# Two attention layers on one core: in the first image's first layer, the residual goes through TensorE and ScalarE, and the last merge of the exponential sums into the column sums

## The chip, the cores and the metric

The kernel runs on one core of a Trainium2 chip. The metric is device time in microseconds (us) for one launch. TensorE is called PE here, its weight loads PEld, VectorE DVE, ScalarE ACT, GpSimd POOL and the DMA queue's engine SP, as in the profile.

## The reference

The input x is four images of 128 channels and 4096 positions, in float32. Two attention layers follow one another; cut to what matters:

```python
# layer 0 (IC = 64), n positions, b images
g = g_w @ x + g_b;  theta = theta_w @ x + theta_b;  phi = phi_w @ x + phi_b
f = softmax(theta^T phi)                # over the keys, 4096 x 4096 per image
x = W_w @ (f @ g) + W_b + x             # residual
# layer 1 (C = 128)
q, k, v = Wq @ x + bq, Wk @ x + bk, Wv @ x + bv
x = x + softmax(q^T k / sqrt(C)) @ v    # residual
```

## The kernel before

Everything stays in float32. The queries of a layer and image are cut into 8 chunks of 512 positions, so there are 64 chunks in all. Their order is the list `chunks`: first the 8 chunks of layer 0 of image 0 (chunks 0 to 7), then chunks of layer 0 of the next image and of layer 1 of the present one by turns. Only the first 8 run with nothing but layer 0 around them.

A chunk takes the 4096 keys in 16 pairs of 128-key tiles. One pair of one chunk is a *slot* t of a software pipeline written out by hand (`slot(t)` under a manual schedule): each engine runs its instructions in the order in which the program issues them. A *turn* is 16 slots. In slot t the program issues, in this order:

- the scores of pair t (PE, L246 for layer 0, into one of two PSUM buffers `ps` of two banks), their copy to an SBUF tile `s` (ACT, L253), the exponential of pair t - 19 in place (ACT, L294), the running sum of that pair's exponentials into `sum` (POOL, L306 for the first addition, L308 for the others), the subtraction of the row maxima from pair t - 18 (DVE, L290), and the running maximum of pair t (DVE, L262, L260 for the first);
- in the odd slots, the value products of two pairs, 20 and 21 slots back (PE, L343 for layer 0);
- the work that comes once per chunk: in slot 0 of the next turn the merge of the maxima (DVE, L265), in slot 1 their transposition, column maximum and spreading (PE L270, DVE L275, PE L282). Chunk g's tail is in turn g + 2: the accumulated values leave PSUM in slot 4 (ACT, L360); `sum_columns` multiplies the exponential sums by a column of ones in slot 7 (PE, `pc`) and `invert` takes the reciprocal (DVE, L373); `sum_spread` and `normalize` are in slot 9 (PE `o_rc`, DVE L381), `project_out` and `residual` in slot 11 (PE `po`, DVE L393). The query projection of a coming chunk is in slot 13 (PE `pq`, ACT L233). `pc`, `o_rc`, `po` and `pq` share one PSUM bank, tag "m".

In the last slots of chunk 7 and after it, the keys and values of the next image (`pk`, `pv`) and of layer 1 come in between.

The exponential sums of a chunk are kept for the two key tiles of a pair side by side, a tile of 128 x 2 x 512. After the last pair, POOL adds the two halves (L311), and `sum_columns` reads only the first half.

`cut` (L187) issues a product as two halves of 64 output columns each when the mode of the slot is "col". While layer 0 is in PE's array the mode is "col", so all of the first eight chunks' `pc` and `po` products are issued in halves. PE's records of a float32 product are two for each half: one `po` is 4 records, one chunk's `pc` (4 blocks of 128 queries) 16.

Scores of layer 0 multiply on 64 rows for each tile of the pair, two products side by side in the array.

Of the kernel before, what the change touches and what calls it, by code (L numbers as in the profile page):

```python
# [11 lines left out]
AF = mybir.ActivationFunctionType  # L12
ALU = mybir.AluOpType
# [4 lines left out]
def kernel(  # L18
# [39 lines left out]
    nc = tc.nc  # L58
    B, C, N = x.shape
    IC = thT.shape[1]  # L60
    P = 128
    NB = 512
    NCH = N // NB
    KT = NB // P
    NPR = N // (2 * P)
# [17 lines left out]
    def const(name, shape):  # L83
        return cp.tile(shape, F32, tag=name, name=name)

    X = {}

    def load(b, j):
        t = xp.tile([C, NB], F32, tag="x", name=f"x_{b}_{j}")
        nc.sync.dma_start(out=t, in_=x[b, :, ts(j, NB)])  # L90
        X[b, j] = t

    ones = const("ones", [P, P])
    nc.gpsimd.memset(ones, 1.0)
    ident = const("ident", [P, P])
# [3 lines left out]
    wq0, wo0 = const("wq0", [P, P]), const("wo0", [P, P])  # L99
    wk0, wv0 = const("wk0", [P, IC]), const("wv0", [P, IC])  # L100
    bq0, bk0 = const("bq0", [P, 1]), const("bk0", [P, 1])
    g0, bo0, wb0 = const("g0", [IC, 1]), const("bo0", [P, 1]), const("wb0", [P, 1])
# [57 lines left out]
    chunks = [(0, 0, c) for c in range(NCH)]  # L160
# [5 lines left out]
    NG = len(chunks)  # L166
# [16 lines left out]
    def cut(out, lhsT, rhs, start=True, stop=True):  # L183

        cols = [slice(0, IC), slice(IC, P)] if now[0] == "col" else [slice(0, P)]
        for c in cols:
            nc.tensor.matmul(out[c], lhsT=lhsT[:, c], rhs=rhs, start=start, stop=stop)  # L187
# [7 lines left out]
    ACC = {}  # L195
    SUM = {}
# [99 lines left out]
    def own(g, p):  # L296

        return g == NG - 1 and p > 0 and p % 3 == 0
# [3 lines left out]
    def sums(g, p):  # L302
        s = S[g, p]
        if p == 1:
            SUM[g] = w2.tile([P, 2, NB], F32, tag="sum", name=f"sum_{g}")
            nc.gpsimd.tensor_tensor(SUM[g], S[g, 0], s, ALU.add)  # L306
        elif p > 1 and not own(g, p):
            nc.gpsimd.tensor_tensor(SUM[g], SUM[g], s, ALU.add)  # L308
        if p == NPR - 1 and g < NG - 1:
            t = SUM[g]  # L310
            nc.gpsimd.tensor_tensor(t[:, 0, :], t[:, 0, :], t[:, 1, :], ALU.add)  # L311

# [17 lines left out]
    def values(g, p):  # L330
# [8 lines left out]
        for h in range(2):  # L339
# [15 lines left out]
            else:  # L355
                nc.tensor.matmul(ACC[g], lhsT=v, rhs=s[:, h, :], start=first, stop=last)  # L356

    def leave(g):
        y = w2.tile([P, NB], F32, tag="y", name=f"y_{g}")
        nc.scalar.copy(y, ACC.pop(g))  # L360
        if g in HI:
            nc.vector.tensor_tensor(y, HI.pop(g)[0], y, ALU.add)
        ACC[g] = y

    def sum_columns(g):
        pc = ps_m.tile([P, KT], F32, tag="m", name=f"pc_{g}")
        for i in range(KT):
            cut(pc[:, i : i + 1], SUM[g][:, 0, ts(i, P)], ones[:, 0:1])
        SUM[g] = pc

    def invert(g):
# [11 lines left out]
    def project_out(g):  # L383
        if chunks[g][0] == 0:
            po = ps_m.tile([P, NB], F32, tag="m", name=f"po_{g}")
            cut(po, wo0, ACC[g])
            ACC[g] = po

    def residual(g):
        layer, b, c = chunks[g]  # L390
        if layer == 0:
            t = X[b, c]
            nc.vector.scalar_tensor_tensor(t, ACC.pop(g), bo0, t, ALU.add, ALU.add)  # L393
        else:
            t = X.pop((b, c))
            nc.vector.scalar_tensor_tensor(t, ACC.pop(g), bv1, t, ALU.add, ALU.add)
            nc.sync.dma_start(out=out[b, :, ts(c, NB)], in_=t)
            if loads:
                load(*loads.pop(0))
# [49 lines left out]
    def slot(t):  # L449
# [6 lines left out]
        if p == 4 and f is not None:  # L456
            leave(f)
        run(scores, of(t, 0))
        run(copy, of(t, 0))
        run(exps, of(t, EL))  # L460
        run(sums, of(t, EL))
        run(subtract, of(t, SL))
        if p == 1 and m is not None:
# [5 lines left out]
        def finish():  # L469
            if t in cols:  # L470
                sum_columns(cols[t])
                invert(cols[t])
            if t in spreads:
                sum_spread(spreads[t])
                normalize(spreads[t])
            if t in outs:
                project_out(outs[t])
                residual(outs[t])
            if t in queries:
                proj_q(queries[t])  # L480
# [56 lines left out]
```

## Time and profile before

| | |
|---|---|
| median of 3 runs | 3079.7 us (3072.96 to 3080.42) |
| profiled execution, its own time | 3076.04 us |
| its span, first to last instruction | 3074.3 us, granted TensorE clock 0.998 |
| PE busy | 3019.3 us, 98% of the span |
| DVE busy | 2532.6 us, 82% |
| ACT busy | 2096.9 us, 68% |
| POOL busy | 2383.8 us, 78% |
| residual of layer 0 (L393) on DVE | 32 in all, 742 ns each (median); those of chunks 0 to 7 start at 109.9 us and later |
| merge of the two halves of the sums (L311) on POOL | 63 in all, 1275 ns each (mean) |

Durations are from one profiled execution. A record's duration includes what overlaps with the next instruction of its engine, so the pitch from start to start is the time that it takes in a row of work. A window query gives the busy time of each engine in a stretch of the span; a wait is listed by who waited for whom, with the total, the number of times and the longest; a line of the timeline has start, duration, engine, source line, operation, output and inputs with shapes, count, and in brackets the idle time before it with its releaser.

### The profile page before, as it was taken

The page shows a single profiled execution, that of the slowest core. Times are in us where ns is not written, and L with a number is a line of the kernel's source. Part 1 is how long each engine was busy: PE and PEld are TensorE (multiplying, and loading weights), DVE is VectorE, ACT ScalarE, POOL GpSimd, SP SyncE. Part 2 cuts the span into 40 slices and gives each one's busy share as a digit, 9 for nine tenths or more (in the row PEclk, how much of TensorE's full clock was granted, in tenths as well). Part 3 has the DMA queues.
Part 4 walks back from the last instruction along what each step waited for, and adds up shares of the span by engine and source line. Part 5 has one row for each costly group of instructions (what it writes and reads, how often), then busy time and mean ns, then how long its engine had stood idle before and what let it go on. Part 6 is the DMA issues. An engine that isn't in the chain of part 4 may idle for free.

```text
span 3074.3 us, 35878 instructions
## 1 busy us (share of the span) xinstructions
PE 3019.3 (98%) x13484; PEld 1243.5 (40%) x13484; DVE 2532.6 (82%) x2337; ACT 2096.9 (68%) x2306; POOL 2383.8 (78%) x1025
## 2 busy tenths in 40 slices
PE   8999999999999999999999999999999999999998
PEld 3222343344443444433344444444333444444444
DVE  6999878888888788888888877888888886766677
ACT  6888867666667676776666776667766676555554
POOL 3999878777888677887878877788878776666667
PEclk9999999999999999999999999999999999999999
DMA  2000000000000000000000000000000000000000
GB/s 67 1 1 1 1 1 8 8 8 4 4 8 8 8 8 1 8 8 8 7 6 2 8 4 4 4 1 4 4 4 4 4 0 4 4 4 7 4 4 11
DMA packets 11534, 19.47 MB, mean 6 GB/s; under 512 B 2656, under 2 KB 3168, under 8 KB 11360
## 3 DMA queue, kind: packets, MB, share of 16 engines
q1 hardware_dynamic: 10896, 17.14, 1.7%
q8 instruction: 106, 1.74, 0.2%
q14 instruction: 68, 0.56, 0.1%
q10 hardware_dynamic: 464, 0.03, 0.0%
HBM read 8.79 MB, written 8.39 MB: 6 GB/s over the span
## 4 chain that ended last, share of the span: by engine, by line
PE 88%; DVE 6%; issue 3%; ACT 3%; POOL 1%; ACTq 0%; DVEq 0%; POOLq 0%
PE ps L187 29%; PE acc L351 15%; PE acc L356 12%; PE ps L246 11%; PE acc L343 11%; DVE mx L262 5%; PE pq L187 2%; ACT s L253 2%; PE pv L187 1%; PE pc L187 1%; PE pt L270 1%; PE o_mx L282 1%; DVE s L290 1%; PE o_rc L282 1%; PE po L187 1%
## 5 line engine op out<-in xcount | busy, mean ns | idle before, releaser
L308 POOL TENSOR_TENSOR sum<-sum,s 128x1024 f32<-128x1024 f32 x891 | 2150.6, 2414 | 494.5 <-ACT s L294 450.9
L253 ACT COPY s<-ps 128x1024 f32<-128x1024 f32 x1024 | 1032.2, 1008 | 853.7 <-PE ps L187 560.4
L262 DVE TENSOR_TENSOR mx<-ps,mx 128x1024 f32<-128x1024 f32 x896 | 1093.9, 1221 | 417.6 <-ACT s L253 417.0
L290 DVE TENSOR_TENSOR s<-s,o_mx 128x1024 f32<-128x1024 f32 x1024 | 1233.2, 1210 | 15.1 <-PE o_mx L282 13.3
L294 ACT ACTIVATE s<-s 128x1024 f32<-128x1024 f32 x1024 | 1090.0, 1065 | 16.5 <-DVE s L290 16.1
L187 PE MATMUL ps<-q,k 128*64 128x512 f32 (+1 forms) x3232 | 929.5, 594 | 2.8 <-ACT k L217 2.8
L246 PE MATMUL ps<-q,k 64*128 64x512 f32 x2048 | 519.3, 613 | 25.4 <-DVE mx L262 24.1
L187 PEld LDWEIGHTS ps<-q,k 128*64 128x64 f32 (+1 forms) x3232 | 325.5, 151 | 506.3 <-issue 445.0
L343 PE MATMUL acc<-s,v 128*64 128x512 f32 x2048 | 497.8, 601 | 8.7 <-ACT s L294 8.7
L352 PE MATMUL hi<-s,v 64*128 64x512 f32 x1104 | 496.0, 589 | 0.0
L351 PE MATMUL acc<-s,v 64*128 64x512 f32 x1104 | 496.0, 589 | 0.0
L356 PE MATMUL acc<-s,v 128*128 128x512 f32 x944 | 424.8, 593 | 0.8 <-ACT y L360 0.7
L351 PEld LDWEIGHTS acc<-s,v 64*128 64x128 f32 x1104 | 205.9, 187 | 260.7 <-issue 202.7
L246 PEld LDWEIGHTS ps<-q,k 64*128 64x128 f32 x2048 | 179.6, 186 | 299.9 <-DVE mx L262 149.1
L306 POOL TENSOR_TENSOR sum<-s,s 128x1024 f32<-128x1024 f32 x64 | 152.1, 2376 | 180.8 <-ACT s L294 180.5
L356 PEld LDWEIGHTS acc<-s,v 128*128 128x128 f32 x944 | 175.3, 190 | 203.3 <-issue 187.4
L343 PEld LDWEIGHTS acc<-s,v 128*64 128x64 f32 x2048 | 131.0, 136 | 279.7 <-issue 157.0
L352 PEld LDWEIGHTS hi<-s,v 64*128 64x128 f32 x1104 | 205.9, 187 | 0.0
L260 DVE TENSOR_TENSOR mx<-ps,s 128x1024 f32<-128x1024 f32 x64 | 78.0, 1218 | 22.5 <-ACT s L253 18.9
L265 DVE TENSOR_TENSOR mx<-mx 128x512 f32<-128x512 f32 x64 | 90.4, 1413 | 2.2
L311 POOL TENSOR_TENSOR sum<-sum 128x512 f32<-128x512 f32 x63 | 80.3, 1275 | 4.9
L187 PE MATMUL pq<-x,wq 128*64 128x512 f32 (+1 forms) x240 | 66.6, 598 | 0.0
(49 smaller groups left out, 846.0 us busy)
## 6 DMA issues: line engine op xcount, KB each, us to landing
x<-in_x_dram SPq DMA_DIRECT2D x32, 256.0 KB, 3.3
out_dram<-x SPq DMA_DIRECT2D x32, 256.0 KB, 2.0
wq<-in_theta_wT_dram SPq DMA_DIRECT2D x2, 32.0 KB, 2.9
wo<-in_W_wT_dram SPq DMA_DIRECT2D x2, 32.0 KB, 4.7
wk<-in_Wk_dram SPq DMA_DIRECT2D x1, 64.0 KB, 2.9
wv<-in_Wv_dram SPq DMA_DIRECT2D x1, 64.0 KB, 2.3
wq<-in_Wq_dram SPq DMA_DIRECT2D x1, 64.0 KB, 1.8
wk<-in_phi_wT_dram ACTq DMA_DIRECT2D x1, 32.0 KB, 3.2
```

Source lines behind the costliest of these rows:

```text
L187: nc.tensor.matmul(out[c], lhsT=lhsT[:, c], rhs=rhs, start=start, stop=stop)
L246: nc.tensor.matmul(ps[:, h, :], lhsT=K[0, b, j][rows, r, :], rhs=q[rows, :], start=True, stop=True)
L253: nc.scalar.copy(s, PS[g, p])
L262: nc.vector.tensor_tensor(M[g], ps, M[g], ALU.max)
L290: nc.vector.tensor_tensor(s, s, BC[g].unsqueeze(1).to_broadcast([P, 2, NB]), ALU.subtract)
L294: nc.scalar.activation(s, s, AF.Exp, scale=scales[chunks[g][0]])
L306: nc.gpsimd.tensor_tensor(SUM[g], S[g, 0], s, ALU.add)
L308: nc.gpsimd.tensor_tensor(SUM[g], SUM[g], s, ALU.add)
L343: nc.tensor.matmul(ACC[g][h * IC : (h + 1) * IC, :], lhsT=v, rhs=s[:, h, :], start=first, stop=last)
L351: nc.tensor.matmul(ACC[g], lhsT=v[lo], rhs=s[lo, h, :], start=first, stop=last)
L352: nc.tensor.matmul(hi, lhsT=v[up], rhs=s[up, h, :], start=(p == p0 and h == 0), stop=(p == p1 and h == 1))
L356: nc.tensor.matmul(ACC[g], lhsT=v, rhs=s[:, h, :], start=first, stop=last)
```

## The change

For chunks 0 to 7 (`alone(g)`: g below NCH = 8):

- `sums` no longer adds the two halves of the exponential sums on POOL.
- `sum_columns` multiplies both halves by the column of ones and sums the products in PSUM: 8 half products per chunk become 16, and 16 records 32.
- `project_out` adds the residual in the array: after the projection, the identity times the chunk's x is summed into the same bank, 4 records more.
- `residual` no longer adds on DVE: ACT evacuates the bank with Identity and the bias bo0 into x.

The other 56 chunks are issued as before; `alone` is false for them.

```diff
-        if p == NPR - 1 and g < NG - 1:
+        if p == NPR - 1 and NCH <= g < NG - 1:
             t = SUM[g]
             nc.gpsimd.tensor_tensor(t[:, 0, :], t[:, 0, :], t[:, 1, :], ALU.add)
...
+    def alone(g):
+
+        return g < NCH
+
...
     def sum_columns(g):
         pc = ps_m.tile([P, KT], F32, tag="m", name=f"pc_{g}")
+        parts = [0, 1] if alone(g) else [0]
         for i in range(KT):
-            cut(pc[:, i : i + 1], SUM[g][:, 0, ts(i, P)], ones[:, 0:1])
+            for h in parts:
+                cut(pc[:, i : i + 1], SUM[g][:, h, ts(i, P)], ones[:, 0:1], h == 0, h == parts[-1])
         SUM[g] = pc
...
             po = ps_m.tile([P, NB], F32, tag="m", name=f"po_{g}")
-            cut(po, wo0, ACC[g])
+            cut(po, wo0, ACC[g], True, not alone(g))
+            if alone(g):
+                cut(po, ident, X[chunks[g][1:]], False, True)
             ACC[g] = po
...
         if layer == 0:
             t = X[b, c]
-            nc.vector.scalar_tensor_tensor(t, ACC.pop(g), bo0, t, ALU.add, ALU.add)
+            if alone(g):
+                nc.scalar.activation(t, ACC.pop(g), AF.Identity, bias=bo0)
+            else:
+                nc.vector.scalar_tensor_tensor(t, ACC.pop(g), bo0, t, ALU.add, ALU.add)
```

## The prediction

> **What bounds the kernel now.** I read the page first: PE is busy for 98% of the span, but the edits touch only chunks 0 to 7, whose tails run in the first 407 us, and there the limits differ. A *turn* is the 16 slots between the first scores of two chunks; the sums, projection and residual of chunk g are in turn g + 2, so turns 2 to 9 change. Busy time in stretches of about one turn, columns PE, PEld, DVE, ACT, POOL (turns 4, 7, 8, 9):
>
> ```profile
> core 0: us, PE busy (x) PEld busy (x) DVE busy (x) ACT busy (x) POOL busy (x), PEclk, DMA share, GB/s
> 157.00:195.50 38.50, 36.07 (x166) 10.68 (x162) 37.53 (x37) 31.31 (x35) 36.94 (x17) 1.00 0.00 1
> 272.50:313.00 40.50, 40.02 (x194) 12.34 (x192) 38.50 (x37) 34.00 (x42) 37.73 (x17) 1.00 0.00 1
> 313.00:353.40 40.40, 39.19 (x267) 14.78 (x267) 38.41 (x38) 38.53 (x49) 37.60 (x17) 1.00 0.00 1
> 353.40:407.00 53.60, 52.20 (x356) 21.60 (x354) 39.42 (x37) 37.20 (x45) 38.28 (x17) 1.00 0.00 1
> ```
>
> Turns 2 to 6 look VectorE-bound, 7 to 9 PE-bound; but PE, VectorE and GpSimd all stand above 93% in turn 4. The waits of turns 4 to 6 (total, times, longest) say who waits there:
>
> ```profile
> PE ps L246 <- DVE mx L262: 5.5, 15, 0.5
> DVE mx L262 <- ACT s L253: 2.2, 3, 0.9
> POOL sum L306 <- ACT s L294: 0.4, 1, 0.4
> ```
>
> PE waits for VectorE 15 times, five in a turn; VectorE waits once, in slot 2. What matters is where in the turn. From the timeline, around the sum columns (slot 7 of turn 4):
>
> ```profile
> 171.77 1.22 DVE L262 TENSOR_TENSOR mx<-ps,mx 128x1024 f32<-128x1024 f32 x1
> 173.04 1.13 PE L246 MATMUL ps<-q,k 64*128 64x512 f32 x4 [0.47 <-DVE mx L262]
> 174.10 0.63 PE L187 MATMUL pc<-ones,sum 128*64 128x1 f32 x16
> 174.59 1.92 PE L343 MATMUL acc<-s,v 128*64 128x512 f32 x8
> 176.44 2.26 PE L246 MATMUL ps<-q,k 64*128 64x512 f32 x8
> 177.52 1.19 DVE L290 TENSOR_TENSOR s<-s,o_mx 128x1024 f32<-128x1024 f32 x1
> 177.67 1.01 ACT L253 COPY s<-ps 128x1024 f32<-128x1024 f32 x1 [1.16 <-PE ps L246]
> 178.71 1.22 DVE L262 TENSOR_TENSOR mx<-ps,mx 128x1024 f32<-128x1024 f32 x1
> ```
>
> A maximum starts only after the copy of the same scores (178.68 to 178.71), and scores start 1.27 after the maximum two slots earlier (171.77, 173.04). VectorE alone would reach max(8) at 177.52 + 1.13 = 178.65; PE brings it at 178.71. So PE's slack at slot 8 is nil, although PE idled 0.47 us three microseconds before. Around the projection (slot 11):
>
> ```profile
> 180.98 1.22 DVE L262 TENSOR_TENSOR mx<-ps,mx 128x1024 f32<-128x1024 f32 x1
> 183.31 1.08 PE L187 MATMUL po<-y,wo 128*64 128x512 f32 x4
> 184.22 1.89 PE L343 MATMUL acc<-s,v 128*64 128x512 f32 x8
> 186.04 1.13 PE L246 MATMUL ps<-q,k 64*128 64x512 f32 x4
> 187.24 0.74 DVE L393 SCALAR_TENSOR_TENSOR x<-po,bo,x 128x512 f32<-128x512 f32 x1
> 187.27 1.01 ACT L253 COPY s<-ps 128x1024 f32<-128x1024 f32 x1 [1.14 <-PE ps L246]
> 189.03 1.22 DVE L262 TENSOR_TENSOR mx<-ps,mx 128x1024 f32<-128x1024 f32 x1
> ```
>
> The copy of scores(12) ends at 188.28, and max(12) starts at 189.03: VectorE is the late one, with the residual in it, by 0.71 us.
>
> **What the Trainium skill says.** "TensorEngine Tiling (Array Packing)", Performance Considerations: a matmul with one moving column costs as much as one with some 60, so the short matmuls aren't free. The trace agrees: 16 records of pc hold PE 0.49 us (174.10 to 174.59), 31 ns each. "TensorE: Matmul & The Clock Gate", opening table: ScalarE's and VectorE's queues are strict FIFO; what stands behind a waiting instruction waits. The trace shows these engines' instructions in program order. "PSUM — Partial Sum Buffer", Terms: two engines may not read one bank at once; this fits the maximum waiting for the copy's end. "ScalarE: Activation LUTs", What ACT_TABLE_LOAD costs: 280 ns + 0.833 ns per element with a per-partition bias, an estimate of 707 ns for 512; the query's Identity (L233, PSUM, same shape and bias form) takes 688, which I use.
>
> **The change part by part.**
> - *VectorE loses the residual.* Start to start 187.24 to 187.90, 0.66 us a turn, eight times.
> - *ScalarE gains it*, 0.69 us. It stands behind exp(11) (185.07 to 186.14) and ahead of copy(12), which waits for PE until 187.27; the projection, even doubled, ends before 186.2. Cost nil; cover: ScalarE's 1.14 us wait for scores(12). In turn 8, ScalarE's fullest (38.53 of 40.4), it idles 0.28 and 0.74 us just there. Were this cover gone, 0.6 us would go on the path of that turn. The bank "m" comes free earlier than by VectorE, so the query projection behind it doesn't wait. Bounds: 0 to 0.6 a turn.
> - *GpSimd loses the merge* (L311): 1.28, 1.4 with its gap. Its sums run without a break for most of a turn, but they caught up with the exponentials (0.38 and 0.42 us idle ahead of L306 at 170.25 and 286.22), and nothing on the path waited for a merge: the sum columns came 4 us after it. Gain 0; at most 0.3, a late copy in turn 4.
> - *PE gains 16 short records per chunk.* The same 16 hold it 0.49 us in turns 2 to 7 and 8, 0.43 in turn 9. Bounds 0.41 (their share on the critical chain of turn 9) and 0.63 (first start to last end).
> - *PE gains 4 records of 128x512.* Like po: 183.31 to 184.22, 0.91; 0.86 in turn 9. Bounds 0.86 and 1.08. The identity and x are long in SBUF; no DMA is issued or moved, and SP's queue is untouched.
>
> *Turns 2 to 6, from one maximum to the next.* Slot 8: PE without slack, so +0.49 for both engines. Slot 12, counted from there: PE brings max(12) at 188.28 + 0.04 + 0.91 = 189.23; VectorE without the residual could start at 188.37. It starts at 189.23, 0.20 later than before: the residual's 0.66 us turn into a wait for PE. Then scores(13) no longer wait for VectorE but follow directly: 186.95 + 1.06 = 188.01 against 187.38, +0.63. The query projection (1.06 after that), values (0.91) and scores(14) (1.81) follow at 191.79; its copy lets max(14) start at 191.79 + 2.28 = 194.07, where VectorE could at 189.23 + 4.53 = 193.76; before it was 193.55. So +0.52 here. Scores(15) start at 192.85, values at 193.9, which wait 0.2 for exp(14); the next turn's scores start at about 195.97 (+0.48), and max(15) and the merge of maxima carry +0.52 into it. A turn grows by 0.49 + 0.52 = 1.01. PE's five waits for VectorE are in slots 1, 5, 7, 13 and 15 (in turn 6: 0.47, 0.43, 0.47, 0.21, 0.27). The last two are used up in the steps above; the first three lie ahead of the added work, behind VectorE's unbroken row of maxima and subtractions, and shift with the end of the turn before. Five turns: +5.1.
>
> *Turns 7 to 9.* Here PE runs without a gap from the sum columns through the projection (VectorE's waits of 0.35 at 294.82 and 0.15 at 305.40 show it), so the whole goes on top: 1.40, 1.40 and 0.43 + 0.86 = 1.29. Together +4.1. VectorE's relief is worth nothing there.
>
> Sum: +9.2. The profiled execution took 3076.04 us (span 3074.3 and 1.7 around it): 3085.2 on its scale. The median of the three runs is 3079.7, 3.7 above that execution; I put the difference on it: **3088.9, rounded 3089**. The bounds of the unseen terms give 7.9 (0.41, 0.86, the late copy gone) to 13.5 (0.63 and 1.08; ScalarE's 0.6 in three turns).
>
> **Rivals.**
> - *PE's gaps absorb the work.* They come to 2.1 us in turn 6, more than 1.4. If scores run ahead so that the gaps move to where the work is, turns 2 to 6 fall by the 0.66, and 7 to 9 keep +4.1: +0.8, 3080.5. Two scores banks forbid running ahead (scores wait for the maximum two slots earlier).
> - *GpSimd sets the pace, the kernel gets faster.* Place: its sums hold the s buffers, and the profile puts 10.0 us of ScalarE's waits for buffers in turns 3 to 7 on them; in the turn from 208.80 to 247.36 it stops for only 0.13 us. Price: 1.4 us in turns 2 to 8, less 1.3 in turn 9: -8.5, 3071. It decides if the sums, not the scores, end last before the copy of slot 2. Against: that copy starts 0.10 after its scores end (201.26 + 1.13, copy at 202.49).
> - *The added matmuls cost more than their neighbours, or ScalarE's order bites.* 0.7 and 1.2 us for them, all on the path of eight turns: +15, 3095. For it: no row shows a group of 32 short records or two products summed by this form. Against: each float32 product is already two records summed in one place.
>
> **How the numbers follow.** Forecast 0.63, gaps absorb 0.14, GpSimd 0.06, dearer matmuls 0.17. A measurement of this kernel can tell about 0.3%, 9.2 us, from no change, and the forecast lies on that line: I put 0.40 of its 0.63 above, as the terms' bounds reach farther up than down. Slower: 0.40 + 0.17 = 0.57. Faster: half of GpSimd's case, 0.03. Same: 0.40. The range of 3079 to 3095 holds the forecast's own range of 3087 to 3093, the absorbing case and most of the dearer one.
>
> **What would show it.** Right: 24 residuals on VectorE instead of 32, 55 merges on GpSimd; turns 3 to 6 at about 39.6 us instead of 38.6, VectorE waiting for copies at slots 8, 12 and 14; turns 7 to 9 longer by 1.3 to 1.4; nothing new after 407 us but the shift. Wrong: turns 3 to 6 at 38 us, or the copy of slot 2 starting earlier against its scores, or a difference that arises after turn 9.

## The result and the profile after

The changed kernel takes 3083.93 us (median of 11 runs, 3079.39 to 3085.41) against 3076.03 us for the kernel before (11 runs, 3072.68 to 3080.42): a ratio of 1.002 on record, with a 95% interval of 1.0012 to 1.0029 (the two medians alone differ by 7.9 us). It is slower by 0.2%, between 4 and 9 us, and stays inside the 0.3% that I had named as the line. The profiled execution has a span of 3079.9 us against 3074.3.

The records are those announced: VectorE's residual of layer 0 (now L404) 24 times instead of 32, GpSimd's merge (L311) 55 times instead of 63, and eight evacuations on ScalarE (L402) of 691 ns each. Lines that kept their number in the trace of before are the same instructions; VectorE's normalization is now L387.

The best yardstick is the *turn*, from one merge of the maxima (L265) to the next, which the timeline gives to 0.02 us. Differences of the start times, in us; the second profile of the kernel before is the experiment e0 below:

| turn | before | before, again | after | after less before, again |
|---|---|---|---|---|
| 1 | 39.98 | 38.46 | 38.45 | 0.0 |
| 2 | 39.17 | 39.17 | 39.91 | +0.74 |
| 3 | 38.55 | 38.55 | 39.33 | +0.78 |
| 4 | 38.83 | 38.82 | 39.31 | +0.49 |
| 5 | 38.56 | 38.55 | 39.33 | +0.78 |
| 6 | 38.57 | 38.56 | 39.33 | +0.77 |
| 7 | 40.16 | 40.16 | 41.51 | +1.35 |
| 8 | 40.22 | 40.22 | 41.55 | +1.33 |
| 9 | 52.73 | 52.74 | 54.06 | +1.32 |

From turn 2 to turn 9 the change costs 7.6 us. After that most turns agree to a few hundredths; five differ by 0.1 or 0.28, and these differences cancel but for 0.1. Turn 4 grew by 0.3 less than its neighbours, because it had been longer by that much before. Turn 1, which holds nothing of the change, was 1.5 us long in the first profile of before alone, where a stretch of 10 us (50 to 60 us) shows a granted clock of 0.83; that is why the two spans differ by only 5.6.

Busy time of the changed kernel in the stretches that answer to those of before (turns 4, 7, 8, 9; columns as there, PE first, then PEld, DVE, ACT, POOL):

```profile
157.00:195.50 38.50, 36.53 (x184) 11.52 (x180) 36.58 (x36) 31.41 (x35) 35.10 (x16) 1.00 0.00 1
275.00:316.50 41.50, 41.04 (x214) 12.85 (x210) 37.51 (x36) 34.34 (x43) 36.17 (x16) 1.00 0.00 1
316.50:358.20 41.70, 40.40 (x288) 15.87 (x288) 37.80 (x37) 39.10 (x49) 36.34 (x16) 1.00 0.00 1
358.20:413.00 54.80, 53.40 (x372) 22.22 (x369) 38.63 (x36) 37.68 (x46) 36.92 (x16) 1.00 0.00 1
```

VectorE's busy time in turn 4 is a microsecond lower (36.58 of 38.5 against 37.53), PE's is higher (36.53 against 36.07). VectorE has become the one that waits. The waits of turns 4 to 6 of the changed kernel (total, times, longest):

```profile
DVE mx L262 <- ACT s L253: 5.6, 9, 0.7
PE ps L246 <- DVE mx L262: 4.9, 12, 0.5
POOL sum L306 <- ACT s L294: 4.4, 3, 1.5
```

Where VectorE waited once in a turn it now waits three times, 5.6 us instead of 2.2 over three turns. GpSimd's wait grew from 0.4 to 4.4: the time that it was given is spent waiting. PE still waits four times in a turn, in turn 5 at slots 1, 5, 7 and 11: the two waits behind the added projection are gone, and one of 0.32 us ahead of it is new.

The timeline of the changed kernel around the sum columns (turn 5, slots 7 and 8):

```profile
212.08 1.13 PE L246 MATMUL ps<-q,k 64*128 64x512 f32 x4 [0.47 <-DVE mx L262]
213.13 1.10 PE L187 MATMUL pc<-ones,sum 128*64 128x1 f32 x32
214.09 1.92 PE L343 MATMUL acc<-s,v 128*64 128x512 f32 x8
215.94 1.99 PE L246 MATMUL ps<-q,k 64*128 64x512 f32 x8
217.17 1.01 ACT L253 COPY s<-ps 128x1024 f32<-128x1024 f32 x1 [1.63 <-PE ps L246]
218.21 1.23 DVE L262 TENSOR_TENSOR mx<-ps,mx 128x1024 f32<-128x1024 f32 x1 [0.47 <-ACT s L253]
```

The 32 short records hold PE 0.96 us (213.13 to 214.09) where 16 held it 0.49, and VectorE's wait at slot 8 is the same 0.47, as the prediction said for this step. From slot 11 on:

```profile
222.81 1.08 PE L187 MATMUL po<-y,wo 128*64 128x512 f32 x4
223.72 1.03 PE L187 MATMUL po<-x,ident 128*64 128x512 f32 x4
224.58 1.89 PE L343 MATMUL acc<-s,v 128*64 128x512 f32 x8
225.25 0.69 ACT L402 ACTIVATE x<-po,bo 128x512 f32<-128x512 f32 x1
226.40 1.99 PE L246 MATMUL ps<-q,k 64*128 64x512 f32 x8
228.31 1.08 PE L187 MATMUL pq<-x,wq 128*64 128x512 f32 x4
228.67 1.22 DVE L262 TENSOR_TENSOR mx<-ps,mx 128x1024 f32<-128x1024 f32 x1 [0.73 <-ACT s L253]
231.04 2.30 PE L246 MATMUL ps<-q,k 64*128 64x512 f32 x8
233.32 1.23 DVE L262 TENSOR_TENSOR mx<-ps,mx 128x1024 f32<-128x1024 f32 x1
```

The identity product takes 0.86 us (223.72 to 224.58). ScalarE's evacuation (225.25 to 225.94) lies ahead of the copy of scores(12), which waits for PE until 227.63, and costs nothing. VectorE waits 0.73 us before max(12): that is where its 0.66 us of residual went. Then comes the difference to the prediction: scores(12) and (13) together take 1.91 us to the start of pq (226.40 to 228.31), where the step had 2.12.

### The profile page after: what moved, and what is told of

Same layout as the page of the kernel before. It is cut to its first block, busy times and chain, and to the rows that moved or that the text cites. A ratio compares the mean times of both kernels' runs of the same rounds, so it can differ in the third digit from the quotient of the medians.

```text
span 3079.9 us, 36189 instructions
## 1 busy us (share of the span) xinstructions
PE 3026.6 (98%) x13644; PEld 1249.7 (41%) x13644; DVE 2515.6 (82%) x2329; ACT 2102.7 (68%) x2314; POOL 2378.5 (77%) x1017
## 4 chain that ended last, share of the span: by engine, by line
PE 89%; DVE 5%; ACT 3%; issue 2%; POOL 1%; ACTq 0%; POOLq 0%; DVEq 0%
PE ps L187 29%; PE acc L351 15%; PE acc L356 12%; PE ps L246 12%; PE acc L343 12%; DVE mx L262 4%; ACT s L253 2%; PE pq L187 2%; PE pc L187 1%; PE pv L187 1%; PE po L187 1%; PE o_rc L282 1%; PE o_mx L282 1%; PE pt L270 1%; POOL sum L308 1%
## 5 line engine op out<-in xcount | busy, mean ns | idle before, releaser
L265 DVE TENSOR_TENSOR mx<-mx 128x512 f32<-128x512 f32 x64 | 77.4, 1210 | 2.2
L311 POOL TENSOR_TENSOR sum<-sum 128x512 f32<-128x512 f32 x55 | 70.0, 1273 | 4.3
L187 PEld LDWEIGHTS pc<-ones,sum 128*64 128x64 f32 (+1 forms) x888 | 55.6, 154 | 27.6 <-issue 21.9
```

## The experiments

Turns 3, 5 and 6 of a run agree to a few hundredths unless told otherwise, so one number stands for them: 38.56 us before, 39.33 changed. They come from one profiled execution of each kernel; the two of the kernel before agree to 0.02 from turn 2 on. "In all" is the growth of the stretch from the start of turn 2 to the end of turn 10 against the kernel before (369.87 us, the mean of its two profiles). Times in single runs scatter by 7 us, so the turns decide. At stake were my theory, that the added work of PE is on the path at the place where it stands while VectorE's and GpSimd's relief becomes waiting, and its rivals: that PE's gaps absorb the work, that relief and cost add up, or that GpSimd sets the pace. The diffs of e1, e2 and e6 are against the changed kernel, those of e3 and e4 against e1, of e5 and e8 against e2, of e10 against e4, of e7 and e9 against the kernel before; `...` marks code left out, and `zeros` is a tile of zeros that is set once at the start.

**e0, the kernel before once more.** No edit.

> The kernel before, unchanged, profiled a second time. My theory: turns 3 to 9 as in the first profile (38.55, 38.5 to 38.8, 38.56, 38.57, 40.16, 40.22, 52.73 us from merge of maxima to merge of maxima), but turn 1 at 38.45 instead of 39.98, because the 1.5 us lost there in the first profile fall in a stretch of 10 us with a granted clock of 0.83, which is chance. Rival: the change itself shortened turn 1 by 1.5 us; then turn 1 is again 39.98.

Turn 1 is 38.46, the others are as in the first profile. In all further profiles but those of e8 and e9, which change its merge, it is 38.45 or 38.46 too. The 1.5 us were chance, and the change didn't shorten anything ahead of its place.

**e1, the residual alone.**

```diff
-        if p == NPR - 1 and NCH <= g < NG - 1:
+        if p == NPR - 1 and g < NG - 1:
...
-        parts = [0, 1] if alone(g) else [0]
+        parts = [0]
```

> Only the residual goes through PE and ScalarE; sum columns and GpSimd's merge as before. My theory (PE has 0.7 us of slack at the projection, VectorE's relief of 0.66 becomes a wait for PE): turns 3 to 6 at 38.8 us against 38.56 before, turns 7 to 9 longer by 0.87 each, about +4.0 us in all. Rival (VectorE bounds turns 2 to 6, PE's gaps take the product): turns 3 to 6 at 37.9, in all -0.7 us.

Turns 3 to 6 at 38.86, turns 7 to 9 longer by 0.88, 0.86 and 0.85, 3.8 in all. No turn became shorter by VectorE's relief, but turn 4, 38.83 before, grew by 0.03 only; e3 shows why.

**e2, the sums alone.** The projection and the residual as before.

```diff
-            if alone(g):
-                cut(po, ident, X[chunks[g][1:]], False, True)
...
-            if alone(g):
-                nc.scalar.activation(t, ACC.pop(g), AF.Identity, bias=bo0)
-            else:
-                nc.vector.scalar_tensor_tensor(t, ACC.pop(g), bo0, t, ALU.add, ALU.add)
+            nc.vector.scalar_tensor_tensor(t, ACC.pop(g), bo0, t, ALU.add, ALU.add)
```

> Only the sums change: GpSimd's merge is gone for chunks 0 to 7, 32 short records instead of 16; the residual stays on VectorE. My theory (no slack on PE at slot 8): turns 3 to 6 at 39.03, turns 7 to 9 longer by 0.47 each, +3.8 us in all. Rival (GpSimd sets the pace, its relief of 1.4 us is worth something): turns 3 to 6 at 38.3 or less.

Turns 3 to 6 at 42.12, 41.39, 41.11 and 41.12, 15.2 us in all: neither theory. Half of the change costs twice as much as the whole. Turns 8 and 9 grew by 0.46, as expected, so the 32 records aren't dearer. The timeline of this kernel at the start of turn 6 shows the place:

```profile
241.21 2.35 POOL L308 TENSOR_TENSOR sum<-sum,s 128x1024 f32<-128x1024 f32 x1
241.31 2.79 DVE L265 TENSOR_TENSOR mx<-mx 128x512 f32<-128x512 f32 x1
```

The merge of the maxima lasts 2.79 us instead of 0.69. It starts 0.10 us after the start of one of GpSimd's additions and ends 0.54 after its end. At the start of turns 3 to 7 it was 2.78 to 2.80 every time. This calls for a theory of its own, tested by e8 and e9.

**e3, PE's product without VectorE's relief.** As e1, but zeros times x is added, and VectorE keeps the residual.

```diff
-                cut(po, ident, X[chunks[g][1:]], False, True)
+                cut(po, zeros, X[chunks[g][1:]], False, True)
...
-            if alone(g):
-                nc.scalar.activation(t, ACC.pop(g), AF.Identity, bias=bo0)
-            else:
-                nc.vector.scalar_tensor_tensor(t, ACC.pop(g), bo0, t, ALU.add, ALU.add)
+            nc.vector.scalar_tensor_tensor(t, ACC.pop(g), bo0, t, ALU.add, ALU.add)
```

> As e1_residual_only, but the extra product is zeros times x and VectorE keeps the residual: PE's cost without VectorE's relief. My theory (the relief is worth nothing once PE is late at slot 12): turns 3 to 6 within 0.1 us of e1_residual_only, 38.8. Rival (relief and cost add up): 0.66 us longer than e1_residual_only, 39.5, 3.3 us in all over five turns.

Turns 3, 5 and 6 at 38.86, the same as e1 to 0.01 (turn 4 at 39.12). VectorE's part of e1 at slot 12, from the subtraction to the maximum:

```profile
223.60 1.21 DVE L290 TENSOR_TENSOR s<-s,o_mx 128x1024 f32<-128x1024 f32 x1
225.54 1.23 DVE L262 TENSOR_TENSOR mx<-ps,mx 128x1024 f32<-128x1024 f32 x1 [0.73 <-ACT s L253]
```

and of e3, the same place, with the residual (L403 there, the other lines moved by two):

```profile
223.62 0.74 DVE L403 SCALAR_TENSOR_TENSOR x<-po,bo,x 128x512 f32<-128x512 f32 x1
224.28 1.21 DVE L292 TENSOR_TENSOR s<-s,o_mx 128x1024 f32<-128x1024 f32 x1
225.56 1.22 DVE L264 TENSOR_TENSOR mx<-ps,mx 128x1024 f32<-128x1024 f32 x1
```

The residual fits exactly into the wait: 223.60 to 225.54 with the wait, 223.62 to 225.56 with the residual. So in these turns the relief of VectorE is worth nothing beside this product of PE, and "relief and cost add up" is wrong. Turn 4 is the exception: there the relief is worth 0.26 (38.86 in e1, 39.12 in e3). Every run that leaves the residual on VectorE has a turn 4 longer than its neighbours by 0.26 to 0.29 (before, e3, e5, e8, e9; e2 against turns 5 and 6), also where GpSimd's merge is gone (e8); no run that takes the residual away has it, also where GpSimd's merge is kept (e1, e4). How the relief does it stays open.

**e4, the relief without PE's cost.** As e1 without the identity product, so these chunks get no residual at all.

```diff
-            cut(po, wo0, ACC[g], True, not alone(g))
-            if alone(g):
-                cut(po, ident, X[chunks[g][1:]], False, True)
+            cut(po, wo0, ACC[g])
```

> VectorE's relief without PE's cost: for chunks 0 to 7 ScalarE evacuates the projection with its bias into x, and x itself isn't added (the residual of the first image's layer 0 is left out). My theory (VectorE is late by 0.71 us at slot 12, PE not far behind it at slot 14): turns 3 to 6 at 38.0 to 38.2 us against 38.56, turns 7 to 9 unchanged, about -2.2 us in all. Rival (GpSimd, whose merge is kept here, sets the pace): 38.4 or more.

Turns 3 to 6 at 38.44 to 38.48, 0.8 us less in all. My theory missed: only 0.1 of the 0.66 us comes through, and 0.36 in turn 4. The timeline of this kernel at slot 14 of turn 5:

```profile
226.30 1.08 PE L187 MATMUL pq<-x,wq 128*64 128x512 f32 x4
227.21 1.89 PE L343 MATMUL acc<-s,v 128*64 128x512 f32 x8
229.02 1.99 PE L246 MATMUL ps<-q,k 64*128 64x512 f32 x8
231.30 1.22 DVE L262 TENSOR_TENSOR mx<-ps,mx 128x1024 f32<-128x1024 f32 x1 [0.47 <-ACT s L253]
```

From the query projection of slot 13 on PE works without a gap, and its scores(14) come so late that max(14) waits 0.47 us for their copy. GpSimd had no wait in turns 3 to 6 of this kernel, so it could also have been the one; e10 tells.

**e5, the short records without GpSimd's relief.** As e2, with GpSimd's merge kept and the second half multiplied by zeros.

```diff
-        if p == NPR - 1 and NCH <= g < NG - 1:
+        if p == NPR - 1 and g < NG - 1:
...
-                cut(pc[:, i : i + 1], SUM[g][:, h, ts(i, P)], ones[:, 0:1], h == 0, h == parts[-1])
+                cut(pc[:, i : i + 1], SUM[g][:, h, ts(i, P)], (zeros if h else ones)[:, 0:1], h == 0, h == parts[-1])
```

> As e2_sums_only, but GpSimd's merge is kept and the second half of the sums is multiplied by zeros: the 32 short records without GpSimd's relief. My theory (the relief is worth nothing): turns 3 to 6 within 0.1 us of e2_sums_only, 39.03. Rival (GpSimd sets the pace): 0.3 us or more longer than e2_sums_only in each turn.

41.13, 41.39, 41.12, 41.12: as e2, with merges of 2.78 to 2.81 us. Turn 3 is even 1 us shorter than in e2. GpSimd's relief is worth nothing here, and the long merge comes with PE's added records, not with GpSimd's missing merge.

**e6, more of it.** The changed kernel with a second product, zeros times x.

```diff
-                cut(po, ident, X[chunks[g][1:]], False, True)
+                cut(po, ident, X[chunks[g][1:]], False, False)
+                cut(po, zeros, X[chunks[g][1:]], False, True)
```

> The changed kernel with a second product, zeros times x, summed into the projection's bank. My theory (in the changed kernel PE is late at slot 12, so nothing hides more work there): turns 3 to 6 at 40.18 us against 39.32 of the changed kernel, turns 7 to 9 longer by 0.86 again, 6.9 us more than the changed kernel and 14.4 more than the kernel before. Rival (PE's gaps still take part of it): half of that in turns 3 to 6, 39.75 or less.

40.17 to 40.18 in turns 3 to 6, turns 7 to 9 longer by another 0.85 to 0.86, 14.4 us in all. The time is 3087.20 us (median of 5) against 3076.09 (17 runs), ratio 1.0037 (1.0024 to 1.0049). The second product's 0.86 us in slot 11 goes on the path whole (0.85 a turn).

**e7, the product where PE had gaps.** For chunks 0 to 4, in halves in slots 3 and 5, into the bank with tag "h".

```diff
+    def identity_half(g, c):
+        if c == 0:
+            PO[g] = ps_a.tile([P, NB], F32, tag="h", name=f"po_{g}")
+        hs = halves[c]
+        nc.tensor.matmul(PO[g][hs], lhsT=ident[:, hs], rhs=X[chunks[g][1:]], start=True, stop=False)
...
+        if p in (3, 5) and f is not None and early(f):
+            identity_half(f, p // 4)
...
```

> The residual through PE and ScalarE for chunks 0 to 4 alone, with the identity product moved ahead: one half of 64 columns in slot 3, one in slot 5, into a bank of its own, where PE waited for VectorE; sums as before. My theory (place decides, not PE's total): each half of 0.43 us meets 0.31 to 0.34 us of slack, and slot 12 gains: turns 3 to 6 at 38.3 to 38.5 us against 38.56 before and 38.8 with the same product in slot 11; in all about -0.8 us against the kernel before. Rival (PE's total work decides): 38.8 as in e1_residual_only.

38.96 to 38.97, 1.8 us in all; 3077.82 us (median of 13) against 3076.09, ratio 1.0006 (0.9998 to 1.0015). My theory missed and the rival came within 0.1 of e1's 38.86: moving the product into these gaps is no better than slot 11. The timeline of this kernel shows where the turn loses, at max(6) and max(14) of turn 5:

```profile
212.94 1.23 DVE L262 TENSOR_TENSOR mx<-ps,mx 128x1024 f32<-128x1024 f32 x1 [0.35 <-ACT s L253]
232.25 1.23 DVE L262 TENSOR_TENSOR mx<-ps,mx 128x1024 f32<-128x1024 f32 x1 [0.47 <-ACT s L253]
```

Max(4) doesn't wait, max(6) does. I read it so that the slack of 0.31 to 0.34 us that I had found at slots 4 and 6 is one and the same: once the half in slot 3 has used it, the half in slot 5 costs VectorE 0.35. A run with one half alone, which would test that, wasn't made. And in slot 14 PE is late as in e4.

**e8, e2 with a merge of one SBUF input.** "SBUF — State Buffer", Who interferes with whom, in the Trainium skill says that a VectorE instruction with two SBUF inputs contends with a GpSimd instruction that reads SBUF and that whichever issued first blocks the other, while a reduction doesn't contend. The merge of the maxima is the only large instruction of a turn on VectorE with both inputs in SBUF.

```diff
-        nc.vector.tensor_tensor(M[g][:, 0, :], M[g][:, 0, :], M[g][:, 1, :], ALU.max)
+        if g < NCH:
+            o = w2.tile([P, 2, NB], F32, tag="mx", name=f"merged_{g}")
+            nc.vector.reduce_max(o[:, 0, :], M[g].rearrange("p h n -> p n h"), AX.X)
+            M[g] = o
...
```

> As e2_sums_only, whose merge of the maxima on VectorE took 2.79 us instead of 0.69 in turns 3 to 7; here the merge is a reduction with one SBUF input (into another buffer of the same pool) instead of an addition-like operation with two. Theory A (an operation with two SBUF inputs waits for GpSimd's running addition to end, a shared SBUF port): the merge takes about 1.2 us, estimated from the 0.69 us of the reduction of 512 elements in the trace and twice the elements, and turns 3 to 6 fall from 41.12 to about 39.5. Theory B (the merge is slow because something else, such as scores or sums, keeps VectorE): turns 3 to 6 at 41 us or more.

In the timeline of this kernel:

```profile
236.27 2.36 POOL L313 TENSOR_TENSOR sum<-sum,s 128x1024 f32<-128x1024 f32 x1
236.37 1.24 DVE L267 TENSOR_REDUCE merged<-mx 128x512 f32<-128x1024 f32 x1
```

The reduction takes 1.24 us though it starts 0.10 after the start of an addition, as the merge in e2 did, and that addition takes its usual 2.36. Turns 3 to 6 are at 39.58, 39.85, 39.58, 39.57: theory A. The rule of the skill agrees with these runs. Less the longer merge (1.24 - 0.69 = 0.55, if all of it is on the path), that is 39.03, the value expected of the sums alone, +0.47; max(8) waits 0.47 in this kernel as in the changed one. With e1's +0.31 it makes 39.34, against the changed kernel's 39.33.

**e9, the kernel before with the merge moved.** One subtraction later in its slot, nothing else.

```diff
-        if p == 0 and m is not None:
-            max_merge(m)
...
         run(subtract, of(t, SL))
+        if p == 0 and m is not None:
+            max_merge(m)
```

> The kernel before with one thing moved: the merge of the maxima is issued behind the first subtraction of its slot instead of ahead of it, about 1.13 us later against GpSimd's additions. Theory A (port): the merge now falls into a running addition and takes about 2.0 us instead of 0.69 in turns 3 to 7, and the turns grow from 38.56 to 39.7 or more. Theory B (no port conflict): the merge stays at 0.69 us and the turns at 38.6 to 39.2, for the later transposition alone.

The merge takes 2.02 to 2.06 us at the start of turns 3 to 7, turns 3 to 6 are 40.49, 40.78, 40.52 and 41.85, and the whole kernel takes 3123.61 us against 3079.89 in single runs. At the start of turn 5:

```profile
199.72 2.36 POOL L308 TENSOR_TENSOR sum<-sum,s 128x1024 f32<-128x1024 f32 x1
200.57 2.06 DVE L265 TENSOR_TENSOR mx<-mx 128x512 f32<-128x512 f32 x1
```

Theory A again: the same instruction is three times as long only by when it starts.

**e10, e4 without GpSimd's merge.** The second half of the sums is left out as well.

```diff
-        if p == NPR - 1 and g < NG - 1:
+        if p == NPR - 1 and NCH <= g < NG - 1:
```

> As e4_relief_only (x isn't added for chunks 0 to 7), and GpSimd's merge of the two halves of the sums is left out too, without the second half in the sum columns. Theory A (in e4_relief_only GpSimd's row of additions, which never stopped, held the turn at 38.46): turns 3 to 6 at 38.2 us or less. Theory B (PE is late at slot 14, GpSimd just keeps up): 38.4 to 38.5 again.

38.45 to 38.48: theory B. GpSimd doesn't set the pace even there. (Turn 8 is 42.10 in this run instead of 40.22, with a merge of 2.90 us at its start: a meeting with an addition once more.)

## Why the prediction was right or wrong

- **Direction and mechanism: right.** PE's additions are on the path, and the relief of VectorE and GpSimd turns into waiting (e1, e3, e5, e6), but for VectorE's 0.28 us in turn 4.
- **Sum columns, +0.49: right.** +0.47 in slot 8 (e8, and VectorE's wait in the changed kernel), 0.46 in turns 8 and 9 (e2).
- **ScalarE nil: right.** The evacuation lies in its wait for PE in every stage, turn 8 too (+1.33 there, not more than in turn 7).
- **Identity product: 0.91 assumed, 0.86 measured.** Two products in a row have the pitch of 0.86, which turn 9 had shown.
- **The step that failed is the one from max(12) to max(14), "+0.52 here".** The identity product with its consequences costs 0.31 a turn (e1). I had let scores(13) follow scores(12) by 1.06 us and pq by another 1.06. In the changed kernel the pair takes 1.91, as it already did in the trace of before where PE was late (slots 2 and 3: 201.26 to 203.17). In before's slots 10 and 11 it took 2.23 (181.08 to 183.31), because the weight loads of the second scores waited 0.88 us for the maximum; in the changed kernel they waited 0.24. The first four lines are of before, the last is of the changed kernel:

```profile
181.08 2.31 PE L246 MATMUL ps<-q,k 64*128 64x512 f32 x8
182.25 0.30 PEld L246 LDWEIGHTS ps<-q,k 64*128 64x128 f32 x4 [0.88 <-DVE mx L262]
201.26 1.99 PE L246 MATMUL ps<-q,k 64*128 64x512 f32 x8
203.17 1.08 PE L343 MATMUL acc<-s,v 128*64 128x512 f32 x4
226.93 0.19 PEld L246 LDWEIGHTS ps<-q,k 64*128 64x128 f32 x2 [0.24 <-DVE mx L262]
```

A PE that is late no longer waits with its loads, and regains 0.2 us. With that, max(14) comes 4.65 us after max(12), 0.12 behind VectorE instead of 0.31. That is 0.19 of the 0.25 a turn by which the step was too large; 0.05 is the pitch of the identity product. Five turns by 0.25 or so (1.01 against 0.76) make 1.3 of the 1.6 us by which the sum was too large. The other 0.3 is turn 4: it was 0.28 longer than its neighbours before and isn't now, the late copy that I had priced at 0.3 at most and taken as nothing. I had put it down to GpSimd's merge; the runs put it down to VectorE's residual (e3).
- **Turns 7 to 9: 4.1 predicted, 4.0 measured.**
- **The base was wrong.** I added the 3.7 us between the profiled execution and the median of three runs. Over 11 runs the median is 3076.03, the profiled execution's own time. On its scale the forecast was 3085.2; the median is 3083.93. So of the 5 us by which the forecast was too high 3.7 are this base.
- **Slower by over 0.3%: not so.** The likeliest value lay on that line with one term too large, and I leaned to the upper side because of unseen costs. None of them arose: 32 short records cost no more per record than 16.
- **GpSimd's rival: wrong**, as argued (e5, e10). But neither the forecast nor any rival had what GpSimd really does to VectorE (e2, e8, e9). The profile of before had the sign of it: the durations of the merge (L265) there go from 691 to 2896 ns, with 21 of 64 at 2.88 or more, all behind the first ten turns, such as this one:

```profile
450.38 2.35 POOL L308 TENSOR_TENSOR sum<-sum,s 128x1024 f32<-128x1024 f32 x1
450.39 2.88 DVE L265 TENSOR_TENSOR mx<-mx 128x512 f32<-128x512 f32 x1
```

In the first turns of before it came just ahead of an addition and took 0.69. In the changed kernel it costs little. There the merge starts 0.18 us ahead of an addition's end (234.65 + 2.37 = 237.02):

```profile
236.84 0.73 DVE L265 TENSOR_TENSOR mx<-mx 128x512 f32<-128x512 f32 x1
237.10 2.71 POOL L308 TENSOR_TENSOR sum<-sum,s 128x1024 f32<-128x1024 f32 x1
```

The merge loses 0.04 us and the next addition 0.34. By the example of e2 I estimate that a third of a microsecond later it would have lost 2.1, in each of five turns. That it didn't was luck, not forecast.

Do such meetings make the spread of the runs of one kernel (7 us)? The profiles say no, but for single cases. In turns 11 to 64 each profile but e9's has 14 to 26 merges of 2.88 to 2.90 us, other ones each time, and where a turn begins with a long merge in one profile and with a short one in another, it takes the same times, to 0.02 us. The exception is one turn of e1 near 2005 us, 1.88 us longer than in the other runs, with such a merge on its critical chain. From the merge that begins turn 11 to the last one the profiles agree to 0.2 us, e1 and e9 apart. What varies lies outside: the first merge starts between 38.4 and 42.0 us, and the span goes on for 49.3 to 53.1 us behind the start of the last one. Why, stays open. A stretch of low granted clock goes with 1.5 us in the first profile of before.

## What to carry to other kernels

Before work is moved from a saturated engine to another, look for the next wait: here taking 0.66 us off VectorE bought nothing in most turns, because the receiving engine, PE, which had 0.71 us of slack at that slot, was due there 0.86 us later. The pitch of PE's instructions told so, not its busy share. Slack read at several slots of one pipeline can be the same slack, to be spent once, as I read it in e7. And when a shift of half a microsecond changes a turn by two, look for an instruction whose own duration has changed before looking for a wait.

## What the runs showed of the hardware

The merge of the maxima, a VectorE operation with both inputs in SBUF, and GpSimd's additions exclude one another for the length of an instruction: one that comes while the other runs is held up until that one ends. The same 128 x 512 merge took 0.69 us where it came ahead of an addition, 2.0 in e9, where it started 0.85 to 0.90 us after the start of one, and 2.8 in e2, 0.1 us after the start of one of 2.35. Wherever it started inside an addition that held it up, in all profiles, it ended 0.54 or 0.55 us after the addition's end. A reduction of one 128 x 1024 input in the same place took 1.24 to 1.26, and VectorE's subtraction and maximum, with one input in PSUM, ran at 1.21 and 1.22 us beside the same additions. GpSimd pays as well: the addition behind a merge takes 2.70 us and more instead of 2.37. The profile shows all this as longer instructions, not as waits. So the phase of two engines that exchange no data can be worth more than the edit under study: 11 us in e2, beyond the 3.8 expected. In e9 it was some 40 us, a part of which is the merge's later place itself.
